# Layer 1 attention: weights normalised before the values, on shared scores, over three graphs at once

## The chip, the cores and the metric

The kernel runs on one core of a Trainium2 chip. The core has TensorE (PE in the profile), VectorE (DVE), ScalarE (ACT), GpSimd (POOL) and the queue engine SyncE (SP), each with its own in-order list of instructions. The metric is the device time of one execution in microseconds; the kernel before took 4247.29 us as the median of three runs (4246.46 to 4250.41).

## The reference

64 graphs of 256 nodes with 512 features pass through two layers. Each layer adds its output to its input and normalises (layer norm).

```python
# layer 0: graph attention, 8 heads of 64 units
feats = einsum('bnf,hfu->bhnu', X, W)
dense = leaky_relu(e_self[..., :, None] + e_neigh[..., None, :], 0.2) + NEG_BIG * (1 - A)
out0  = relu(softmax(dense) @ feats + b)
x = layernorm(x + out0)
# layer 1: dot-product attention with two matrices that all heads share, 8 heads of 64
dots = where(m2, q @ k.T * 64**-0.5, -big)          # m2: both nodes in the mask
attn = softmax(dots) * 0.33
attn = attn + 0.33 * where(m2, adj, 0) + 0.33 * exp(-where(m2, adj, big))
x = layernorm(x + (attn @ v) @ W_out + b_out)
```

The part of `attn` after the softmax depends on the graph and not on the head. The kernel calls it `ct`, stored transposed (keys along the partitions, queries along the free axis). A row of the softmax that the mask empties is spread evenly in the reference; that share (0.33/256) is added to `ct`.

## The kernel before

All tensors are float32. Per graph there are two blocks of 128 nodes (`T = 2`), four blocks of 128 features (`C = 4`) and four pairs of heads (`HG = 4`).

Work is written as lists of steps with weights. `together` (L507) merges such lists: it always takes the step whose list has advanced least. A scheduler in the build then fixes the order of instructions on each engine and hoists loads as far ahead as their buffers allow. For each `b`, the loop at L525 merges two times. First `attend0(b)` with the first part of `proj1(b-1)`; then `attend1(b-1)` with `proj0(b+1)`.

`proj0` (L199) transposes x, forms the features of layer 0 (`pf`, L290), the logits (`pe`), their rows (`pr`, L259) and `ct` from the adjacency (`pa`, L215). `rows` sends a row of 8 KB out to DRAM (`gs`, L273) and loads it back into all partitions (`gb`, L274); `nd`, `ccol` and `wcol` (L279 to L285) wait for it, and `scaled` (L300, GpSimd) waits for `wcol`. The mask is cast to float on GpSimd (L225), which frees the buffer that a later mask load (L78) waits for.

`attend0` (L321) forms each head's weights on VectorE (`pT`, L329, two per head) and multiplies by the features in `weighted` (L161).

`proj1` (L367) transposes the normalised input (`pt_h`), forms queries and keys per pair of heads (`pq`, L377), copied by ACT, and the values `v` (`pv`, L391), with a column of ones at the end of each head, so that a product with unnormalised weights also gives their sum.

`attend1` (L408) does, per pair of heads: `scores` (L413), where the two heads' products sit in the upper and the lower 64 rows of TensorE (`pz`, L419), and ACT takes the exponential (L428). `values` (L434) uses `weighted` with the unnormalised exponentials as the stationary operand and 65 columns of `v` as the moving one, then takes the maximum with a tiny number, the reciprocal, the mask factor and a product on VectorE (L437 to L440). `rest` (L448) multiplies `ct` by all heads' values once (`pcv`, L451), and `combine` (L460) adds it on GpSimd. The sum is transposed (`pt_o`), copied to `oT` by ACT, and `project` (L471) multiplies by W_out (`po`, L474). `end` normalises and stores.

PSUM tiles come from tags: `mm`, `tr` and `av` with two buffers each, `sc` (the scores) with one.

## Time and profile before

| | |
|---|---|
| median of three runs | 4247.29 us (4246.46 to 4250.41) |
| the profiled execution | 4250.41 us, span 4248.3 us |
| granted TensorE clock, mean | 0.993 |
| TensorE busy | 4059.7 us, 96% |
| VectorE busy | 1575.9 us, 37% |
| ScalarE busy | 1030.5 us, 24% |
| GpSimd busy | 961.5 us, 23% |
| DMA | 163.50 MB, mean 38 GB/s |

The profile is one execution. Busy time is the union of an engine's instructions; a matmul's end is modelled, so a row's mean duration overlaps the next one, and the distance between starts is what a matmul costs in a stream. PEld is TensorE's loading of the stationary operand. In a row of groups, the numbers after the bar are the busy time in us, the mean of one in ns, then the idle time of the engine ahead of these instructions and what ended it. A row of a timeline has the start in us, the length in us, engine, line, operation, what is written and read, the shapes, how many instructions are merged, and in brackets the idle time ahead. The queue of SP issues nearly all DMAs.

### The profile page before, as it was taken

The numbers are of one execution on the slowest core, as the hardware profiler recorded it, in microseconds if no ns is written. First come the engines' busy times: TensorE is split into PE (matmuls) and PEld (weight loads), VectorE is DVE, ScalarE is ACT, GpSimd is POOL, SyncE is SP. The second block draws the span as 40 slices with busy tenths as digits, with TensorE's granted clock in tenths as the row PEclk, the third lists the DMA queues.
The fourth block names the chain that finished last, engine by engine and source line by source line (L and its number), as shares of the span: only waits on it lengthen the run. The fifth ranks groups of instructions, "written<-read, shape, count | busy, mean of one in ns | idle before, by whom it ended". The sixth has DMA issues, their size and how long they took to land.

```text
span 4248.3 us, 51561 instructions
## 1 busy us (share of the span) xinstructions
PE 4059.7 (96%) x20994; PEld 2867.6 (67%) x20994; DVE 1575.9 (37%) x4123; ACT 1030.5 (24%) x1857; POOL 961.5 (23%) x1414
## 2 busy tenths in 40 slices
PE   6999999999999999999999999999999999999998
PEld 4676676666766766667667666676676766766765
DVE  4334334343343343433433434334334343343342
ACT  1222222222222222222222222222222222222222
POOL 2222222122222221222222212212222122122221
PEclk9999999999999999999999999999999999999999
DMA  4101101011011110111111101101111011011000
GB/s 119 36 33 41 41 33 41 29 46 36 34 41 41 33 41 28 46 36 33 41 41 33 41 29 46 36 33 41 41 33 41 29 46 36 33 41 40 26 31 10
DMA packets 89739, 163.50 MB, mean 38 GB/s; under 512 B 30624, under 2 KB 47520, under 8 KB 81312
## 3 DMA queue, kind: packets, MB, share of 16 engines
q1 hardware_dynamic: 76208, 155.49, 11.1%
q10 hardware_dynamic: 13296, 4.72, 0.5%
q8 instruction: 166, 2.72, 0.3%
q14 instruction: 69, 0.57, 0.0%
HBM read 126.11 MB, written 34.08 MB: 38 GB/s over the span
## 4 chain that ended last, share of the span: by engine, by line
PE 91%; POOL 4%; DVE 3%; issue 1%; DMA 1%; ACT 0%; POOLq 0%; DVEq 0%; ACTq 0%; SPq 0%
PE pq L377 21%; PE av_h L167 21%; PE pv L391 11%; PE pf L290 10%; PE po L474 9%; PE pz L419 6%; PE pcv L451 5%; PE pe L246 3%; POOL o L461 2%; PE pt_x L154 1%; PE pt_h L154 1%; PE pt_o L154 1%; DVE ct L227 1%; POOL ct L240 1%; DVE ct L223 1%
## 5 line engine op out<-in xcount | busy, mean ns | idle before, releaser
L377 PE MATMUL pq<-hT,wqkv_sb 128*128 128x256 f32 x4096 | 940.6, 383 | 0.7 <-ACT hT L157 0.7
L377 PEld LDWEIGHTS pq<-hT,wqkv_sb 128*128 128x128 f32 x4096 | 759.5, 190 | 93.1 <-ACT hT L157 1.0
L461 POOL TENSOR_TENSOR o<-o,cv 128x512 f32<-128x512 f32 x128 | 161.7, 1263 | 1766.0 <-DVE o L440 1766.0
L329 DVE SCALAR_TENSOR_TENSOR pT<-gb,ccol,at 128x256 f32<-128x256 f32 x1024 | 529.4, 570 | 40.5 <-PE av_h L167 40.0
L474 PE MATMUL po<-wo_sb,oT 128*128 128x512 f32 x1024 | 495.8, 619 | 41.9 <-ACT oT L157 41.9
L167 PEld LDWEIGHTS av_h<-v,p 128*128 128x128 f32 x4096 | 482.0, 192 | 53.1 <-issue 51.8
L167 PEld LDWEIGHTS av_h<-v,pT 128*128 128x128 f32 x4096 | 493.1, 192 | 14.4 <-POOL v L305 3.1
L167 PE MATMUL av_h<-v,p 128*128 128x65 f32 x4096 | 491.7, 274 | 0.0
L167 PE MATMUL av_h<-v,pT 128*128 128x65 f32 x4096 | 486.1, 272 | 2.2 <-POOL v L305 2.2
L290 PE MATMUL pf<-w_sb,xT 128*128 128x512 f32 x1024 | 467.9, 599 | 0.0
L391 PE MATMUL pv<-wqkv_sb,hT 128*128 128x512 f32 x1024 | 466.1, 598 | 0.0
L386 ACT COPY qk<-pq 128x512 f32<-128x512 f32 x256 | 149.9, 585 | 1184.1 <-PE pq L377 1184.1
L428 ACT ACTIVATE p<-pz,hide 128x512 f32<-128x512 f32 x512 | 323.7, 683 | 251.0 <-PE pz L419 251.0
L348 POOL TENSOR_TENSOR o<-o,b_bc 128x256 f32<-128x256 f32 x256 | 196.5, 768 | 793.3 <-DVE o L343 793.3
L474 PEld LDWEIGHTS po<-wo_sb,oT 128*128 128x128 f32 x1024 | 189.7, 195 | 248.7 <-issue 192.1
L437 DVE TENSOR_SCALAR rec<-av_h 128x4 f32<-128x4 f32 x256 | 41.4, 162 | 829.2 <-PE av_h L167 829.2
L290 PEld LDWEIGHTS pf<-w_sb,xT 128*128 128x128 f32 x1024 | 190.4, 192 | 212.4 <-issue 212.4
L391 PEld LDWEIGHTS pv<-wqkv_sb,hT 128*128 128x128 f32 x1024 | 184.8, 191 | 184.9 <-issue 184.9
L419 PE MATMUL pz<-qk 64*128 64x256 f32 x2048 | 290.4, 402 | 0.0
L419 PEld LDWEIGHTS pz<-qk 64*128 64x128 f32 x2048 | 176.4, 186 | 133.9 <-issue 118.2
L451 PE MATMUL pcv<-v,ct 128*128 128x512 f32 x512 | 236.9, 605 | 0.0
L481 DVE TENSOR_TENSOR x<-po,x 128x512 f32<-128x512 f32 x128 | 87.7, 685 | 338.1 <-PE po L474 338.1
(70 smaller groups left out, 3060.9 us busy)
## 6 DMA issues: line engine op xcount, KB each, us to landing
gb<-gs SPq DMA_DIRECT2D x64, 1028.0 KB
x<-in_x_dram SPq DMA_DIRECT2D x64, 512.0 KB, 3.6
out_dram<-y SPq DMA_DIRECT2D x64, 512.0 KB, 2.8
adj<-in_adj_dram SPq DMA_DIRECT2D x64, 256.0 KB, 2.7
wqkv_sb<-in_L_gnn_W_qkv_dram ACTq DMA_DIRECT2D x12, 256.0 KB, 6.8
mask<-in_nodemask_dram SPq DMA_DIRECT2D x64, 32.0 KB, 2.9
w_sb<-in_L_gnn_W_dram SPq DMA_DIRECT2D x4, 256.0 KB
wo_sb<-in_L_gnn_W_out_dram ACTq DMA_DIRECT2D x1, 1024.0 KB
```

The costliest lines, as they stand in the source:

```text
L167: nc.tensor.matmul(av[:, k, :], weights[h][:, j, t * P : (t + 1) * P], v[:, j, h, :], start=(j == 0), stop=(j == T - 1),)
L290: nc.tensor.matmul(pf, xT[:, c, t * P : (t + 1) * P], w0_sb[:, c].rearrange("p h u -> p (h u)"), start=(c == 0), stop=(c == C - 1),)
L329: nc.vector.scalar_tensor_tensor(pT[h][:, j, :], GB[b][:, h, :N], CCOL[b][:, j, h : h + 1], AT[b][:, j, :], op0=ALU.max, op1=ALU.mult,)
L348: nc.gpsimd.tensor_add(o[:, t, s], o[:, t, s], b0_bc[:, s])
L377: nc.tensor.matmul(pq[:, s, :], wqkv_sb[:, c, s, 2 * g : 2 * g + 2, :].rearrange("p h u -> p (h u)"), hT[:, c, :], start=(c == 0), stop=(c ...
L386: nc.scalar.copy(QK[b][:, g], pq)
L391: nc.tensor.matmul(pv, hT[:, c, t * P : (t + 1) * P], wqkv_sb[:, c, 2].rearrange("p h u -> p (h u)"), start=(c == 0), stop=(c == C - 1),)
L419: nc.tensor.matmul(pz[:, r, j, :], QK[b][rows, g, 1, j * P : (j + 1) * P], QK[b][rows, g, 0, :], start=True, stop=True,)
L428: nc.scalar.activation(p[:, :, j, :], pz[:, :, j, :], AF.Exp, bias=hide[:, j, b : b + 1])
L451: nc.tensor.matmul(pc, CT[b][:, j, t * P : (t + 1) * P], V1[b][:, j, :, :U], start=(j == 0), stop=(j == T - 1),)
L461: nc.gpsimd.tensor_add(o[:, t, :], o[:, t, :], cv[:, t, :])
L474: nc.tensor.matmul(po, oT[:, c, t * P : (t + 1) * P], wo_sb[:, c, :], start=(c == 0), stop=(c == C - 1),)
```

## The change

1. Layer 1's softmax becomes a list of its own, `softmax1`. It has the scores and exponentials as before. VectorE then adds the two key blocks of each pair (`both`). TensorE sums over the partitions with a block of 32 columns of the constant 1/0.33 as stationary operand; the four heads of two pairs go to the four column quarters (`sums`). VectorE takes the reciprocal of that (128x512, from PSUM) and multiplies by the query mask. One partition of every quarter is sent to DRAM (`rs`) and loaded back into all partitions (`rb`, 128 x 8 KB).
2. `attend1` starts with `weights`: GpSimd multiplies each head's exponentials by its row of `rb`, VectorE adds `ct`. Each is an operation on 128x512, eight per graph on either engine.
3. Its `values` takes the values of one head (64 columns) as the stationary operand and 256 columns of finished weights as the moving one; the two heads of a pair go to the two column halves of TensorE. The result is already transposed, so ACT copies it to `oT` directly. `rest`, `combine`, the transposes of `o` and the column of ones fall away.
4. The loop merges `attend1(b-2)`, `attend0(b)` and `proj1(b-1)`, and then `softmax1(b-1)` with `proj0(b+1)`. It runs one turn longer.
5. Buffers: `p` 5 in place of 3, `ct` 4 in place of 3; `gb`, `qk` and `o` one in place of two; the float mask row is kept in `mf` with three buffers.

```diff
+    ones = consts.tile([P, P // 4], FT, name="ones")
+    nc.vector.memset(ones, 1.0 / LA)
...
-            prod = work.tile([P, H, U], FT, tag="o", name=f"prod_{c}_{s}")
+            prod = work.tile([P, H, U], FT, tag="o", name=f"prod_{c}_{s}", bufs=1)
...
-        GB[b] = work.tile([P, H, N + 1], FT, tag="gb", name=f"gb_{b}")
+        GB[b] = work.tile([P, H, N + 1], FT, tag="gb", name=f"gb_{b}", bufs=1)
...
-        CT[b] = work.tile([P, T, N], FT, tag="ct", name=f"ct_{b}", bufs=3)
+        CT[b] = work.tile([P, T, N], FT, tag="ct", name=f"ct_{b}", bufs=4)
...
-            mrow = small.tile([P, N], FT, tag="mrow", name=f"mrow_{b}", bufs=2)
+            mrow = MF[b] = small.tile([P, N], FT, tag="mf", name=f"mf_{b}", bufs=3)
             nc.gpsimd.tensor_copy(mrow, MROW[b])
...
-        QK[b] = work.tile([P, HG, 2, N], FT, tag="qk", name=f"qk_{b}")
-        V1[b] = work.tile([P, T, H, UA], FT, tag="v1", name=f"v1_{b}")
+        QK[b] = work.tile([P, HG, 2, N], FT, tag="qk", name=f"qk_{b}", bufs=1)
+        V1[b] = work.tile([P, T, H, U], FT, tag="v1", name=f"v1_{b}")
...
+            both[g] = work.tile([P, 2, N], FT, tag="both", name=f"both_{b}_{g}", bufs=3)
+            nc.vector.scalar_tensor_tensor(
+                both[g], p[:, :, 0, :], TINY, p[:, :, 1, :], op0=ALU.add, op1=ALU.add
+            )
...
+        def sums(pd, g):
+            for r in range(2):
+                k = 2 * (g % 2) + r
+                nc.tensor.matmul(
+                    pd[k * 32 : (k + 1) * 32, g // 2, :],
+                    ones,
+                    both[g][:, r, :],
+                    start=True,
+                    stop=True,
+                    tile_position=(0, 32 * k),
+                )
+        def reciprocals():
+            pd = ps_tile([P, 2, N], "av", f"pd_{b}")
+            for g in range(HG):
+                sums(pd, g)
+            rec = work.tile([P, 2, N], FT, tag="rec1", name=f"rec1_{b}", bufs=1)
+            nc.vector.reciprocal(rec, pd)
             nc.vector.tensor_mul(
+                rec, rec, MF[b].unsqueeze(1).to_broadcast([P, 2, N])
+            )
+            rs = dram.tile([4, 2, N], FT, tag="rs", name=f"rs_{b}")
+            nc.sync.dma_start(rs, rec[0:P:32])
+            nc.sync.dma_start(
+                REC[b].rearrange("p k g n -> p (k g n)"),
+                rs.rearrange("k g n -> (k g n)").partition_broadcast(P),
+            )
...
+        def weights(g):
+            p = PROBS[b][g]
+            for r in range(2):
+                k = 2 * (g % 2) + r
+                nc.gpsimd.tensor_mul(
+                    p[:, r],
+                    p[:, r],
+                    REC[b][:, k, g // 2, :].unsqueeze(1).to_broadcast([P, T, N]),
+                )
+                nc.vector.tensor_add(p[:, r], p[:, r], CT[b])
+        def values(g):
+            if g % 2 == 0:
+                av[0] = ps_tile([P, 2, N], "av", f"av1_{b}_{g}")
+            for j in range(T):
+                for r in range(2):
+                    nc.tensor.matmul(
+                        av[0][r * U : (r + 1) * U, g % 2, :],
+                        V1[b][:, j, 2 * g + r, :],
+                        PROBS[b][g][:, r, j, :],
+                        start=(j == 0),
+                        stop=(j == T - 1),
+                    )
+            if g % 2 == 1:
+                nc.scalar.copy(oT[:, g - 1 : g + 1, :], av[0])
...
-    for b in range(NB + 1):
+    for b in range(NB + 2):
         if b + 2 < NB:
             load(b + 2)
-        first, then = proj1(b - 1) if b >= 1 else ([], [])
-        together(attend0(b) if b < NB else [], first)
         together(
-            attend1(b - 1, then) if b >= 1 else [],
+            attend1(b - 2) if 0 <= b - 2 < NB else [],
+            attend0(b) if b < NB else [],
+            proj1(b - 1) if 0 <= b - 1 < NB else [],
+        )
+        together(
+            softmax1(b - 1) if 0 <= b - 1 < NB else [],
             proj0(b + 1) if b + 1 < NB else [],
         )
```

## The prediction

> **What bounds the kernel now.** I read the busy times first, then the chain of waits, then one graph's stretch of the timeline, engine by engine, then the DMA queue's own waits. On the page, busy times and chain:

> ```profile
> PE 4059.7 (96%) x20994; PEld 2867.6 (67%) x20994; DVE 1575.9 (37%) x4123; ACT 1030.5 (24%) x1857; POOL 961.5 (23%) x1414
> ...
> PE 91%; POOL 4%; DVE 3%; issue 1%; DMA 1%; ACT 0%; POOLq 0%; DVEq 0%; ACTq 0%; SPq 0%
> ```

> TensorE is the bound. From one rows() step to the next (L264 starts at 2153.16, one graph later at 2218.5) a graph takes 65.3 us. TensorE's timeline gives the pitches that I use (start to next start), and the only place where it stands idle:

> ```profile
> 2108.38 3.67 PE L377 MATMUL pq<-hT,wqkv_sb 128*128 128x256 f32 x16
> 2111.89 1.90 PE L167 MATMUL av_h<-v,pT 128*128 128x65 f32 x16
> ...
> 2133.23 1.13 PE L419 MATMUL pz<-qk 64*128 64x256 f32 x8
> 2134.29 1.96 PE L246 MATMUL pe<-wa,xT 128*128 128x16 f32 x16
> ...
> 2148.99 3.70 PE L451 MATMUL pcv<-v,ct 128*128 128x512 f32 x8
> ...
> 2157.52 0.66 PE L154 MATMUL pt_o<-ident,o 128*128 128x128 f32 x4 [0.48 <-POOL o L461]
> 2158.85 1.98 PE L474 MATMUL po<-wo_sb,oT 128*128 128x512 f32 x4 [0.67 <-ACT oT L157]
> 2162.00 0.66 PE L154 MATMUL pt_o<-ident,o 128*128 128x128 f32 x4 [1.17 <-POOL o L461]
> ```

> A float32 matmul is two records. 16 of pq take 3.51 (0.219 each), 16 of av_h 1.73, 8 of pz, whose two heads sit in different row halves, 1.06 (0.133 each: they overlap), 8 of 512 columns about 3.5, 16 of pe 1.8, four transposes 0.44.

> VectorE and GpSimd get in each other's way:

> ```profile
> 2165.63 1.04 POOL L300 TENSOR_TENSOR v<-feat,wcol 128x512 f32<-128x512 f32 x1 [3.34 <-ACT wcol L285]
> 2165.75 1.20 DVE L329 SCALAR_TENSOR_TENSOR pT<-gb,ccol,at 128x256 f32<-128x256 f32 x1
> 2166.97 5.25 DVE L329 SCALAR_TENSOR_TENSOR pT<-gb,ccol,at 128x256 f32<-128x256 f32 x11
> ```

> A pT step costs 0.47 (pitch 0.40), but the one that meets L300 ends only 0.28 after it.

> SP's own queue has a wait that costs nothing today (columns: us in total, times, longest): a later graph's mask load stands until GpSimd's cast has emptied its buffer.

> ```profile
> SPq L78 <- POOL mrow L225: 302.1, 58, 5.4
> ```

> [...]no run shows column tiles. [...]On 4 elements it takes 182 ns from PSUM against 162 for the maximum beside it (L341, L437)[...]. [...]here a stretch of 3.4 us at 2420.3, after one in which TensorE was busy 2.24 of 3.4 us, shows a granted 0.50.

> **TensorE's work per graph.** Removed: 64 records av_h from p (6.9), pcv (3.5), pt_o (0.9) and its idle time (2.3). Unchanged: transposes 1.8, pq 14.0, pz 4.3, layer 0's av_h 6.9, po and pv 7.0 each, pe 1.8, pf 7.0, pr and pa 0.9: 50.8. Added: the values, 8 heads x 2 blocks x 2 records of 256 columns in alternating column halves. Between 0.133 each as pz (4.3) and 0.219 as pq (7.0); I take 4.3[...]. The sums: 16 records, between 1.2 (four quarters at once) and 3.5 (none); I take 2.0. TensorE alone would need 57.1, a gain of 8.

> **The new wait.** I count from E, the end of a graph's sums. In the order that the build fixes, TensorE then has pt_h, a half of pt_x, three pq groups (10.5), the other half of pt_x, half a pz group, then the first of layer 1's values. With a wait for ACT's hT copies it gets there at E+13.3. Those values need, one after another:

> The reciprocal over 128x512 of PSUM, from E+0.25. Lower end 0.68 (L481, an addition from PSUM); [...]the 20 and 33 ns that 4 elements cost over other operations give 6.6 ns an element more, so 4.1. It ends at 4.35. nd (0.17) and the multiplication by the mask (0.69) end at 5.2. nd's gb landed before: gs leaves at E-5.35, gb follows 1.33 later and lands some 6.9 after its issue (traffic of the one issued at 2156.6 stops at 2163.4), E+2.9.

> rs leaves at 5.25 and lands 1.3 later, as gs does. But SP's queue has the next graphs' mask load between rs and rb. It waits for the mask cast, and GpSimd's queue has that behind both v steps, which wait for wcol, so for nd. Here nd, ccol and wcol, the v steps, the cast, the mask load and rb all stand in line. From 5.2: v 1.04, copy 0.39, one pT let in 0.28, v 1.04, pT 0.28, copy 0.39, cast 0.40: 9.0; the mask's issue 0.38: 9.4. rb leaves 2.8 later than it could. It moves 1 MB as gb does (6.8; first graphs 5.5): landed at 16.3.

> Then 8 multiplications on GpSimd (1.26 each, as L461 in place with two full tiles; lower end 1.04, L300) and 8 additions on VectorE, both with two SBUF inputs, taking turns: 8 x 1.26 + 7 x 0.55 ([...]from the 0.28 of 256) + 0.6 = 14.5, and 0.4 for layer 0's normalisation, which stands between the last additions. Without turns 10.7. The first pair's weights are ready at 21.2, the next at 24.8 and 28.4, the last at 31.2. TensorE stands idle from 13.3 to 21.4, and again before every pair, av_h and half a pz being all that lies between.

> Values of the last pair end at 31.4 + 1.06 = 32.5. After them, until the next E, 38.0 of TensorE's own work with its operands ready: av_h 5.2, po 7.0, a pq 3.5, pv 7.0, pe 1.8, pz 3.2, pf 7.0, pr and pa 0.9, transposes and sums 2.4. Period 70.5. [...]the clock halves each time; most of that falls into later waits, and I add 1.2 for the part that doesn't (nothing to 3.4): 71.7 against 65.3.

> **Edits at no cost.** VectorE loses 4.0 a graph (L437 to L440) and gains 8 additions (5), 4 sums of blocks (2.8), the reciprocal and a multiplication: 25 + 9 of 71, still idle in between; GpSimd's 15.0 become 22. ACT loses cv and copies oT as before. Single buffers of gb, qk and o: their last readers end a phase before the next writer; without that cover gb alone would cost its 6.9. prod's single buffer is in the setup, whose steps are all VectorE's. The added 64 MB take the first queue from 11% to about 16%.

> **Sum.** Span before: 4248.3 = 83 up to the first full graph, 62 x 65.3, and 58 + 59 for the last two. After: 83, a graph without attend1 47, 61 x 71.7 = 4374, then 61 without the next proj0, 55 without layer 0, and a last attend1 behind its own chain 47: 4667. The profiled execution took 4250.4, 3 above the median of its three runs, and 2 above its span; against the median I say 4660.

> **Rivals.** (a) A shorter chain, still exposed: no turns takes 3.9 off a graph, 4430; a mask load that lets rb go at once 2.8, 4500[...]. Against it: the 1.20 above, and the queue orders. (b) Column halves that don't overlap: 0.7 at the last pair and 1.5 in the sums, 4800; the earlier pairs hide in the waits. For it: no run shows a column tile. (c) Faster: the stage of 14.5 is the place. If GpSimd multiplies by a broadcast row at its one-input rate (L236: 256 elements in 0.40, so 0.75) and VectorE's additions slip in beside it, it takes 6.6, the period is 63.8 and the time 4180. It decides below 7.8. For it, L300, which has a broadcast operand, is 1.04 and not 1.26; against it, that operand is constant along the inner axis and this one isn't. (d) No difference: the stage lands near 7.8 by chance.

> **Chances.** The case forecast, 4520 to 4800: 0.60. (a) 0.20, 4270 to 4520. (b) 0.10, 4800 to 4950. (c) 0.08, (d) 0.02. 4380 to 4850 leaves out the lower half of (a), half of (b), and (c): two in ten. Faster by over 0.2% 0.08, within 0.2% 0.02, slower 0.90; 0.2% is about what a measurement of this kernel can tell.

> **What would show it.** TensorE's share falls to about 80%, with idle time before the values ended by DVE's addition; GpSimd waits for rb; SP's rb issue follows the mask issue at once; the reciprocal near 4 us; additions with a mean over 1 us; the values near 0.13 us a record; a clock of 0.5 in each graph. A reciprocal near 0.7 and additions near 0.6 with the multiplications back to back would make me wrong.

## The result, and the profile after

The changed kernel takes 4429.94 us (median of four runs, 4428.51 to 4433.36) against 4246.88 us for the kernel before (four runs). The ratio is 1.043, with a 95% interval of 1.041 to 1.045: 183 us slower, where the forecast was 413 us slower. Direction and range hold; the forecast size was more than double the measured one.

On the page of the changed kernel, these are the span, the busy times, the granted TensorE clock over 40 slices and three groups (busy us, mean ns of one, then idle time before and what ended it):

```profile
span 4427.2 us, 47399 instructions
...
PE 4015.2 (91%) x18946; PEld 2591.0 (59%) x18946; DVE 2576.9 (58%) x3995; ACT 951.2 (21%) x1729; POOL 1665.8 (38%) x1670
...
PEclk9998989989989889898898998988988989889998
...
L493 DVE TENSOR_TENSOR p<-p,ct 128x512 f32<-128x512 f32 x512 | 795.6, 1602 | 314.1 <-POOL p L488 314.1
L488 POOL TENSOR_TENSOR p<-p,rb 128x512 f32<-128x512 f32 x512 | 801.7, 1601 | 422.6 <-DMA rb<-rs 422.6
...
L501 PE MATMUL av<-p,v 128*64 128x256 f32 x2048 | 469.9, 534 | 334.4 <-DVE p L493 334.2
```

The reader sees the predicted line of waits: TensorE's values (L501) wait for VectorE's additions, these for GpSimd's multiplications, these for `rb`. Multiplications and additions take 1.60 us each. The clock is no longer near full (mean granted 0.910, against 0.993 before). TensorE's busy time has hardly fallen, although it has 2,048 matmul records less.

The waits by engine (us in total, times, longest), from three answers of the trace for the changed kernel, show the same, and SyncE's wait that keeps `rb` back:

```profile
PE av L501 <- DVE p L493: 334.2, 148, 13.8
...
SPq L82 <- POOL mf L229: 161.0, 58, 2.8
...
POOL p L488 <- DMA rb<-rs: 422.6, 64, 17.8
```

One graph of the changed kernel in the timeline (start, length, engine, line, what; idle time ahead in brackets). Its sums end at E = 2177.44, the next graph's at 2245.63:

```profile
2177.56 3.36 DVE L462 RECIPROCAL rec<-pd 128x512 f32<-128x512 f32 x1 [0.73 <-PE pd L448]
...
2181.67 0.51 SPq L467 DMA_DIRECT2D rs<-rec  x1
...
2184.41 0.65 POOL L229 CAST mf<-mask 128x256 f32<-128x256 uint8 x1
2185.09 0.34 SPq L82 DMA_DIRECT2D mask<-in_nodemask_dram  x1
...
2185.53 0.38 SPq L468 DMA_DIRECT2D rb<-rs  x1
...
2189.98 0.70 PE L426 MATMUL pz<-qk 64*128 64x256 f32 x4
...
2191.83 12.53 POOL L488 TENSOR_TENSOR p<-p,rb 128x512 f32<-128x512 f32 x8 [6.22 <-DMA rb<-rs]
2193.12 10.11 DVE L493 TENSOR_TENSOR p<-p,ct 128x512 f32<-128x512 f32 x6 [4.88 <-POOL p L488]
2194.91 1.11 PE L501 MATMUL av<-p,v 128*64 128x256 f32 x2 [4.23 <-DVE p L493]
...
2198.48 3.68 PE L171 MATMUL av_h<-v,pT 128*128 128x65 f32 x16
...
2205.14 2.64 PE L501 MATMUL av<-p,v 128*64 128x256 f32 x16
```

Every link of the predicted chain is there, in the predicted order: `rs`, the cast, the mask load, `rb`, then the stage of eight and eight. TensorE arrives at the first values at 2190.7 and waits 4.2 us. After that it hardly waits: 16 records of `av_h` take 3.68 us here, where they took 1.90 before. It works at half clock: the granted clock is 0.50 from about 15.3 us after E to 29 us after E in this graph and nearly all others. Two stretches of this graph show it, the first inside that time and the second behind it (the granted clock is the third number from the end):

```profile
core 0: us, PE busy (x) PEld busy (x) DVE busy (x) ACT busy (x) POOL busy (x), PEclk, DMA share, GB/s
2192.90:2203.10 10.20, 7.63 (x30) 5.16 (x32) 9.98 (x6) 0.00 (x0) 10.20 (x8) 0.50 0.01 2
...
2206.50:2216.50 10.00, 10.00 (x53) 7.06 (x50) 4.42 (x10) 0.62 (x2) 0.90 (x1) 0.99 0.00 0
```

Times after E, means over 45 graphs of the changed kernel, against the steps of the prediction:

| after E, us | predicted | measured |
|---|---|---|
| reciprocal ends | 4.35 | 3.48 |
| `rs` issued | 5.25 | 4.24 |
| cast ends | 9.0 | 7.62 |
| `rb` issued | 9.4 | 8.08 |
| TensorE reaches the first values | 13.3 | 13.25 |
| first multiplication | 16.3 | 14.76 |
| first pair's weights ready | 21.2 | 19.46 |
| last weights ready | 31.2 | 28.76 |
| last values end | 32.5 | 30.4 |
| next E | 71.7 | 68.27 |

### The profile page after: what moved, and what is told of

Read it like the earlier page. It is cut to its first block, busy times and chain, and to the rows that moved or that the text cites. A ratio compares the mean times of both kernels' runs of the same rounds, so it can differ in the third digit from the quotient of the medians.

```text
span 4427.2 us, 47399 instructions
## 1 busy us (share of the span) xinstructions
PE 4015.2 (91%) x18946; PEld 2591.0 (59%) x18946; DVE 2576.9 (58%) x3995; ACT 951.2 (21%) x1729; POOL 1665.8 (38%) x1670
## 5 line engine op out<-in xcount | busy, mean ns | idle before, releaser
L493 DVE TENSOR_TENSOR p<-p,ct 128x512 f32<-128x512 f32 x512 | 795.6, 1602 | 314.1 <-POOL p L488 314.1
L488 POOL TENSOR_TENSOR p<-p,rb 128x512 f32<-128x512 f32 x512 | 801.7, 1601 | 422.6 <-DMA rb<-rs 422.6
L382 PEld LDWEIGHTS pq<-hT,wqkv_sb 128*128 128x128 f32 x4096 | 773.4, 190 | 136.1 <-issue 31.4
L501 PE MATMUL av<-p,v 128*64 128x256 f32 x2048 | 469.9, 534 | 334.4 <-DVE p L493 334.2
L171 PEld LDWEIGHTS av_h<-v,pT 128*128 128x128 f32 x4096 | 582.3, 223 | 105.6 <-issue 67.6
L171 PE MATMUL av_h<-v,pT 128*128 128x65 f32 x4096 | 596.1, 307 | 0.6 <-POOL v L310 0.6
L353 POOL TENSOR_TENSOR o<-o,b_bc 128x256 f32<-128x256 f32 x256 | 220.5, 862 | 803.6 <-DVE o L348 803.6
L501 PEld LDWEIGHTS av<-p,v 128*64 128x64 f32 x2048 | 193.9, 186 | 553.9 <-DVE p L493 418.4
L518 PE MATMUL po<-wo_sb,oT 128*128 128x512 f32 x1024 | 463.8, 596 | 0.0
L426 PE MATMUL pz<-qk 64*128 64x256 f32 x2048 | 338.6, 440 | 2.2 <-ACT p L435 2.2
L245 POOL TENSOR_TENSOR ct<-ct,even 128x256 f32<-128x256 f32 x128 | 101.2, 809 | 553.4 <-DVE ct L231 550.5
L188 POOL TENSOR_SCALAR rstd_l<-mv_l 128x2 f32<-128x2 f32 x128 | 28.2, 220 | 714.1 <-DVE mv_l L186 714.1
```

The source lines that it names most:

```text
L171: nc.tensor.matmul(av[:, k, :], weights[h][:, j, t * P : (t + 1) * P], v[:, j, h, :], start=(j == 0), stop=(j == T - 1),)
L353: nc.gpsimd.tensor_add(o[:, t, s], o[:, t, s], b0_bc[:, s])
L382: nc.tensor.matmul(pq[:, s, :], wqkv_sb[:, c, s, 2 * g : 2 * g + 2, :].rearrange("p h u -> p (h u)"), hT[:, c, :], start=(c == 0), stop=(c ...
L426: nc.tensor.matmul(pz[:, r, j, :], QK[b][rows, g, 1, j * P : (j + 1) * P], QK[b][rows, g, 0, :], start=True, stop=True,)
L488: nc.gpsimd.tensor_mul(p[:, r], p[:, r], REC[b][:, k, g // 2, :].unsqueeze(1).to_broadcast([P, T, N]),)
L493: nc.vector.tensor_add(p[:, r], p[:, r], CT[b])
```

## The experiments

Two theories go through the experiments. Theory 1: the chain from the sums through `rs`, `rb`, the multiplications and the additions sets when the values end, and the rest of the graph follows. Theory 2: something else is the price, mostly TensorE's halved clock; where a run's text gives it another meaning, that holds. Periods are medians of the graphs in the middle of a run; 4427 us of span belong to a period of 68.25. e1, e2, e3, e6, e7 and e9 were run once; where a kernel was run four times, its runs lie within 0.2% of one another.

**e1: the mask's loads on GpSimd's queue.** SyncE no longer waits between `rs` and `rb`.

```diff
-        nc.sync.dma_start(MROW[b], nodemask[b].partition_broadcast(P))
+        nc.gpsimd.dma_start(MROW[b], nodemask[b].partition_broadcast(P))
```

> The mask loads go to GpSimd's queue, nothing else changes. Theory 1 (the line from the sums over reciprocal, rs, rb and the turns of GpSimd and VectorE sets a graph's time, microsecond for microsecond): rb leaves when rs has landed, some 2.4 us earlier, the period falls from 68.2 to about 65.8 and the time to about 4280. Theory 2 (what costs is TensorE's halved clock, whatever the length of the wait): the gap stays long enough to halve the clock, TensorE stays the slower one behind it, and the time falls by less than half of that, above 4350.

Measured: 4194.4 us (one run), 53 below the kernel before. The build lays TensorE's instructions as in the changed kernel, so the two compare step by step. `rb` is issued at E+5.97 instead of 8.08, and the first multiplication starts at 10.63 instead of 14.79: 2.1 us from the queue and another 2.0 because `rb` flies faster. In the changed kernel the mask's 128 packets of 256 bytes fall from 0.5 to 3.6 us after `rb`'s issue, and `rb`'s last packet lands 6.3 us after it; here it is 4.3. The last weights are ready 4.1 us earlier (24.70) and the period is 4.6 shorter (63.68).

From the page and the waits of this run:

```profile
PE 3902.0 (93%) x18946; PEld 2503.8 (60%) x18946; DVE 2604.5 (62%) x3995; ACT 951.1 (23%) x1729; POOL 1709.0 (41%) x1734
...
PEclk9999999999999999999999999999999999999998
...
PE av L501 <- DVE p L493: 206.4, 268, 14.0
```

The clock holds in most graphs (mean granted 0.973), and 268 waits of TensorE stand where there were 148: at full clock TensorE does wait before the later pairs, 3.4 us in all per graph. A few graphs here fall to half clock, and they are a comparison within one run. At full clock the last value record starts 0.75 us after the last addition, at half clock 1.70; in both the next E follows 38.22 us after that record, as it does in the changed kernel. So the halved clock of the changed kernel costs at most 0.95 us a graph (on average 0.5, since it mostly ends just then): it fills time in which TensorE would have waited. Theory 1 stands: the period falls by the 4.1 us of the chain and these 0.5. That is nearly twice the expected 2.4, because the flight was shortened as well.

**e2: the additions left out.** VectorE doesn't add `ct`; that part of the computation is missing.

```diff
-                nc.vector.tensor_add(p[:, r], p[:, r], CT[b])
```

> VectorE's addition of ct to the weights is left out, so the shared matrices are missing from layer 1. Theory 1 with turns[...]: the multiplications go from 1.7 us each to 1.26 and the stage from 14.0 us to about 10.1; if TensorE keeps up, the period falls by 3.9 and the time to about 4185. Theory 2: TensorE works at half clock in this stretch and can't use the earlier weights; the stage shortens, but the period by about 2 only, 4300. If the two engines don't hinder each other, the multiplications keep their 1.7 us and only the last addition's 0.7 is saved, 4385.

Measured: 4313.75 us. The multiplications' group on the page:

```profile
L488 POOL TENSOR_TENSOR p<-p,rb 128x512 f32<-128x512 f32 x512 | 629.2, 1265 | 431.8 <-DMA rb<-rs 431.8
```

1265 ns in place of 1601: the taking turns is shown. The weights are ready 4.1 us earlier (24.66), but the period falls only 1.4 (to 66.9). The last values now start 2.5 us after the weights are ready instead of 1.2, because TensorE at half clock (10.2 us in a graph) is behind; and the build laid a whole `pz` group and a transpose behind the values, so that 39.7 us follow instead of 38.2. The stage's 4.1 is thus eaten by 1.3 and 1.5. Theory 1's 4185 is out, and theory 2's 4300 is close: with the stage shorter, TensorE at half clock is part of what holds the values back. The build's other order is as large a part, and no theory had it.

**e3: the reciprocal twice.**

```diff
             nc.vector.reciprocal(rec, pd)
+            nc.vector.reciprocal(rec, pd)
```

> The reciprocal is done twice into the same tile. Theory 1: one more time 3.36 us on the line in every graph, period 71.6, time about 4640. Theory 2: the longer gap costs itself but the clock is already halved, the same to within 20 us. If the line isn't what sets the end (other work is), the time moves by less than 60 us.

Measured: 4537.78 us, 108 slower. That is about half of what theory 1 expected, and neither of the other two forecasts holds. The two groups of this run:

```profile
L462 DVE RECIPROCAL rec<-pd 128x512 f32<-128x512 f32 x64 | 214.9, 3358 | 46.6 <-PE pd L448 46.6
L463 DVE RECIPROCAL rec<-pd 128x512 f32<-128x512 f32 x64 | 214.9, 3357 | 0.4
```

The second one costs its 3.36 us on VectorE, and `rs` leaves 3.57 later. But the build put `nd` ahead of it, so the `v` steps and the cast run under it: `rb` leaves only 1.5 later, and lands 4.8 us after its issue instead of 6.3, with the mask's packets over by 1.65. The first multiplication starts when it did before (14.7). What the added time costs comes later: the last weights 0.6, the last values 1.0, and in some graphs a clock that stays halved until E+37 or E+40, with 3 to 4.5 us more behind the values. So a longer reciprocal isn't a longer chain by the same amount. The build also put more of `pz` ahead of the values, so that TensorE reaches them at 16.2 instead of 13.2. The experiment tells little on the chain's slope; that is in e1.

**e4: the values behind everything that doesn't need them.** `attend1` forms all weights first, and its value products get a lead, so that the build lays them behind layer 0's products and the projections.

```diff
         steps = []
-        for g in range(HG):
-            steps += [(0, lambda g=g: weights(g)), (0.9, lambda g=g: values(g))]
+        steps += [(0, lambda g=g: weights(g)) for g in range(HG)]
+        steps += [(100.0, lambda: None)]
+        steps += [(0.9, lambda g=g: values(g)) for g in range(HG)]
```

> Same work, other order: layer 1's values are put behind all of the next graphs' projections and layer 0's products, so that 26 us of TensorE's work stand between the sums and the first value in place of 13. Theory 1: the line is covered, TensorE's own 57 to 58 us and some small waits (layer 0's weights behind the reciprocal) set the period, 58 to 62, time 3750 to 3950, clock back above 0.98. A rival in which VectorE and GpSimd[...] are the true bound: period above 65, time above 4200. Theory 2 alone (clock, not the wait) expects the same as theory 1 only if the clock comes back.

Measured: 4060.33 us (4059.45 to 4062.83); the ratio to the kernel before is 0.956 (0.954 to 0.958). The chain is as slow as ever (first multiplication at E+15.5, last weights at 29.2) and no longer decides: the first values are reached at 27.6. The page, the waits, and two rows of TensorE's timeline:

```profile
PE 3756.9 (93%) x18946; PEld 2438.7 (60%) x18946; DVE 2611.7 (64%) x3995; ACT 957.0 (24%) x1729; POOL 1652.4 (41%) x1670
...
PEclk9999999999999999999999999999999999999998
...
PE av L501 <- DVE o L348: 145.7, 62, 3.5
...
2021.75 1.95 PE L501 MATMUL av<-p,v 128*64 128x256 f32 x16 [2.32 <-DVE o L348]
2023.63 3.70 PE L396 MATMUL pv<-wqkv_sb,hT 128*128 128x512 f32 x8
```

The same 18946 matmul records take 258 us less busy time here than in the changed kernel, and the mean granted clock is 0.984 instead of 0.910. Period 61.31, of which 57.8 are TensorE's own work, 2.3 a new wait and 1.2 small ones. The new wait is for a PSUM buffer: layer 0's normalisation (L348), which empties it, stands behind the additions in VectorE's queue.

The period and the clock are as theory 1 had them; the time is 110 us above the range that was given with it. The rival is out: VectorE and GpSimd hold each other up here as before (13.7 us from the first multiplication to the last weights, 14.0 in the changed kernel), and the period is not above 65.

**e5: values last, and the mask on GpSimd's queue.** The edits of e1 and e4 together.

> Layer 1's values last (as in e4_values_last) and the mask's loads on GpSimd's queue (as in e1_mask_queue). Theory 1 (the chain rs, rb, multiplications, additions decides until TensorE has work enough to cover it): with the values last the chain is covered but for 2.3 us at the first values, where the chain delays VectorE's layer 0 normalisation, which holds the av buffer. The mask's move makes the chain about 4 us earlier, so those 2.3 us go: period about 59 against 61.3, 3900 to 3950 us. Theory 2 (those 2.3 us come from VectorE's own amount of work and not from the chain): same as e4_values_last within 20 us, about 4060.

Measured: 4059.59 us (4055.98 to 4062.58), ratio 0.956 (0.955 to 0.958): the same as without the mask's move. Theory 1 was wrong here, and the number of theory 2 holds. `rb` leaves at E+6.0, and the first multiplication starts at 15.5 all the same. GpSimd's timeline for one graph of this run (E = 1989.46) tells why:

```profile
1997.57 0.64 POOL L82 DMA_DIRECT2D mask<-in_nodemask_dram  x1
2000.62 0.89 POOL L353 TENSOR_TENSOR o<-o,b_bc 128x256 f32<-128x256 f32 x1 [2.40 <-DVE o L348]
2004.12 0.90 POOL L353 TENSOR_TENSOR o<-o,b_bc 128x256 f32<-128x256 f32 x1 [2.62 <-DVE o L348]
2004.98 12.53 POOL L488 TENSOR_TENSOR p<-p,rb 128x512 f32<-128x512 f32 x8
```

With layer 0 ahead, its bias addition (L353) stands before the multiplications in GpSimd's queue and waits for VectorE. The multiplications follow it without a gap, so `rb` has long landed: the chain has another last link.

**e8 and e10: a shorter lead.** A lead of 30 instead of 100, with the mask on GpSimd's queue, and with it on SyncE's.

> As e5_values_last_mask_queue, but the values are held back by a lead of 30 instead of 100, so that they lie among the projections and layer 0's products rather than behind all of them. If the chain's cover is all that counts, 30 is enough once the mask is out of the chain (first values wanted about 25 us after the sums): within 30 us of e5. If the av buffers' order counts more, it is slower than e5 by over 1%.

> As e8_lead30_mask_queue with the mask's loads back on SyncE's queue. Theory 1 (with layer 0 ahead of the values, the first multiplication stands behind layer 0's bias addition in GpSimd's queue, at 15.5 us after the sums, and no longer behind rb, so the mask's place is worth nothing): within 10 us of e8_lead30_mask_queue, 4022 to 4042 us. Theory 2 (e8's gain over e5 is the mask's move showing at a shorter lead): 4060 us or more.

Measured: 4031.25 us (4028.49 to 4033.66, ratio 0.949, 0.948 to 0.951) and 4030.47 us (4029.27 to 4034.51, ratio 0.949, 0.948 to 0.951). The mask's place is worth nothing in this order, as theory 1 had it. The lead is worth 28 us against e5, just inside the 30 us expected: TensorE reaches the first pair's values at E+22.3, when they are ready, and the wait for the PSUM buffer, now before the second half, is 1.9 instead of 2.3. From e8's waits:

```profile
PE av L501 <- DVE o L348: 117.7, 62, 1.9
```

These two are the fastest. The version with a lead of 30 and nothing else changed is 217 us below the kernel before and 399 below the changed one.

**e6 and e7: TensorE work in the gap.** Twelve products that nobody reads, in each graph, meant to fill the wait before the first values and keep the clock.

```diff
+        def warm():
+            pw = ps_tile([P, 2, N], "av", f"pw_{b}")
+            for k in range(12):
+                nc.tensor.matmul(
+                    pw[:, 0, :],
+                    ident,
+                    wqkv_sb[:, k % 4, 0, :4, :].rearrange("p h u -> p (h u)"),
+                    start=True,
+                    stop=True,
+                )
-        steps = []
+        steps = [(0, warm)]
```

> The changed kernel with 12 more TensorE multiplications (128x256, products that nobody reads) in each graph, about 5.2 us of TensorE work, laid in the wait before the first values. Theory 1 (the wait for the first values sets the period, the halved clock after it costs only a little): the filler fills a wait and changes nothing, period about 68, 4400 to 4430 us. Theory 2 (the halved clock that follows the wait is what costs): with the wait filled, the time at half clock goes from 13.7 us a graph to under 3, and the run falls below 4250 us.

> As e6_clock_filler, and the additions of the edge weights to the layer 1 weights are left out (so that part of the computation is missing). Theory 1 (multiplications and additions hold each other up[...], and the values wait for them): with the clock kept, the stage of 8 multiplications falls from 14.1 to about 10.5 us, and the period by 3.5 against e6_clock_filler, about 64, 4180 us. Theory 2 (TensorE's own work is the bound once the clock is kept): within 40 us of e6_clock_filler.

Measured: 4796.63 us, and 4617.07 us with the additions left out. In e6 both theories missed. Its page:

```profile
L501 PE MATMUL av<-p,v 128*64 128x256 f32 x2048 | 470.0, 542 | 324.2 <-DVE p L493 324.2
...
L534 PE MATMUL pw<-wqkv_sb,ident 128*128 128x256 f32 x1536 | 366.8, 388 | 0.0
```

The filler costs its whole time and the wait is as long as before. The build keeps the amount of work ahead of the values: with the filler there, it laid a `pq` group, four transposes and half a `pz` group behind the values. From the last value record to the next E it is now 43.16 us instead of 38.22, and the period grows by 5.7 (medians). So the wait wasn't filled, and the test says nothing on the clock. That the run grew by the work pushed behind the values is what theory 1 says of the part after them. With the additions left out, the weights are ready 4.3 us earlier and the period falls by 2.2 (medians), 180 us in all. That rules out theory 2's 40 us. Theory 1's 3.5 us isn't reached either, and it was forecast for a clock that is kept, which it is in neither run (means of 0.916 and 0.939).

**e9: half of the value products.** Of each head's two key blocks only the first is multiplied by the values; that part of the computation is missing.

```diff
-            for j in range(T):
+            for j in range(1):
...
-                        stop=(j == T - 1),
+                        stop=(True),
```

> The changed kernel with half of layer 1's value products left out (the second 128 nodes of each head: 16 of a graph's 32 TensorE records; that part of the computation is missing). They take 0.117 us each at full clock, 0.234 at half clock, so 1.9 to 3.7 us a graph. Theory 1 (the chain through the multiplications and additions sets when the values end, TensorE is ahead of it even at half clock, and the halved clock costs next to nothing): only the records after the last addition count, period shorter by 0.3 to 0.7 us, 4385 to 4410 us. Theory 2 (TensorE at half clock paces the stage of the values): period shorter by 1.9 to 3.7 us, 4200 to 4315 us.

Measured: 4515.38 us, 85 slower with less work, which neither theory had. The page:

```profile
PEclk9888988989889888898888988888889889888998
...
L501 PE MATMUL av<-p,v 128*64 128x256 f32 x1024 | 408.6, 630 | 325.6 <-DVE p L493 324.6
```

The chain's times are unchanged (first multiplication 14.7, last weights 28.9). The clock isn't: in most graphs it stays at half until 36 or 37 us after E instead of 29, so that 8 us of the work behind the values run at half speed. Within this run, graphs whose clock returns at E+27 have periods of 66.0 to 66.8, those where it returns at E+36 or later have 70.4 to 71.7; the order of TensorE's records is the same in all of them. In the first kind the last values again come 0.9 us after the last addition, and 36.9 us follow instead of 38.2, six `av_h` products having moved ahead of the last values: the chain decides there as theory 1 says. In the second kind the halved clock costs some 4.5 us. So it is cheap in the changed kernel only because it happens to end with the stage.

## Why the prediction was right or wrong

**The kind of bound: right.** TensorE was the bound, and the change takes work off it: 57.8 us a graph at full clock in e4 against the predicted 57.1. The values take 3.8 there (4.3 predicted) and the sums 1.55 (2.0), so the rest was put 1.6 too low. But the values now wait for a chain over five queues, and the period is that chain plus the 38 us that come after it. The 38.0 predicted for that part was measured as 38.2 from the start of the last record. In e1 the same 38.22 follow a chain 4.1 us shorter, and e4 shows that with the chain covered the same instructions take 370 us less.

**The mask load between `rs` and `rb`: right, and undersized.** Predicted 2.8 for the queue; e1 gave 2.1 from it and 2.0 more from the flight, which the prediction had put at 6.9 with no thought of the mask's packets ahead of it.

**The sizes: wrong, nearly all on one side.** The path was right; what failed is the size of three terms of the period. Predicted period 71.7, measured 68.27; 3.4 x 61 is 209 of the 240 us between the predicted and the measured span. Nearly all of the other 31 lie at the end of the run: the last four full periods are 63.7 to 65.3, and the last graphs behind them take 149 us where the sum had 163. The 3.4 are 1.5 up to the first multiplication, 0.9 in the stage of eight and eight and 1.2 for the clock, less 0.2 behind the last weights:

- The reciprocal. "6.6 ns an element more", an estimate from operations on 4 elements, was put on top of an element's normal rate, which gave 4.1 us. It took 3.36, or (3358 - 182)/508 = 6.25 ns an element in all. An addition from PSUM takes some 1.03 ns an element ((685 - 162)/508, from L481 and L437 of the kernel before), so the sum had 7.6 ns in all, which the measurement corrects: the reciprocal takes about six times what the addition does. Of the two differences that were averaged, the like pair (on 4 elements, 182 ns for the reciprocal against 162 for the maximum, both from PSUM) alone gives 20/4 + 1.03 = 6.0 ns and about 3.25 us; the 33 ns, for which the prediction shows no line, made the estimate too long. With an earlier start and a shorter line of `v` steps and cast, `rb` left 1.3 earlier than forecast, and flew 0.2 less.
- The turns. A multiplication with an addition in turn takes 1.67 us, not 1.26 + 0.55 = 1.81, and the first two multiplications are not held up (1.26 and 1.27 us in the graph shown). The stage took 14.0 instead of 14.9. e2 shows that it is the two engines that hold each other up (1265 ns without additions).
- The clock. 1.2 us was added for what the halving doesn't hide. e1 puts it at 0.5 on average, and the term for the last pair (1.3) already held nearly that much. The wait in which the clock falls is 4.6 us on average, not 8.1: besides the earlier weights, TensorE starts with the first head at E+17.8, when one addition is done, where the sum had it wait for the pair. Where the halving would show was also wrong: "idle again before every pair" was forecast, but TensorE at half clock is as slow as the weights come, so only the first wait is left and TensorE's share is 91%, not about 80%. e1's full-clock graphs have the forecast waits.

**The rivals.** The time lies in the range of (a), a chain that is shorter but still exposed, which was given 0.20, and not in the 4520 to 4800 of the case forecast. That its 4430 is the measured time is luck: its reason, no turns, is wrong, as the turns are there, and in its place three terms and the end of the run came out shorter at once. (b), column halves that don't overlap, is out: 0.117 us a record in e4 against 0.219 for a record of 256 columns that fills the array. Ahead of the result, their overlap was an estimate from the row halves of `pz` (0.133 us a record). (c) needed a stage below 7.8 us and (d) one near it; it took 14.0. The way to a faster kernel was not the stage but the order of TensorE's work.

**What stays open.** Why `rb` flies 2 us longer behind the mask's packets: its 128 packets are the same and take 0.37 us each against 0.34, and a mask packet itself takes 15 ns, so the packets' own time doesn't explain it. Where the packets of the mask are over sooner, 1.65 us after `rb`'s issue in e3, `rb` lands after 4.8, which fits, but no run shows the mechanism. Open too is why the clock stays halved for 13.65 us in the changed kernel (49 of its 61 falls) and until E+36 or E+37 in most graphs of e9. The filler that should have settled the clock's cost by itself was moved out of the way by the build.

## What to carry to other kernels

When a change puts a chain over several queues ahead of an engine's next operand, the gain in that engine's work counts only if other work of that engine, in its program order, covers the chain: here 22 us of cover in place of 13 (e10) turned a loss of 4% into a gain of 5%. Look first at what lies between two DMA issues of the chain on their queue, and ask of every link what will be last once it is removed. Filler or less work can move the order or the clock and make things worse (e6 and e9 take 367 and 85 us more than the changed kernel), so the order has to be read again after every edit.
